# An SSM and FP8 FFN kernel: another cut of the last outputs, another order of the last products

## Chip, cores, metric

The kernel runs on one core of a Trainium2 chip. The metric is device time in microseconds (us). Three runs of the kernel before gave 304.72 to 305.21 us, median 305.06. A core has TensorE (PE, matrix products), VectorE (DVE), ScalarE (ACT), GpSimd (POOL) and SyncE (SP), each with an instruction queue of its own; SP and GpSimd also issue the DMAs, which 16 DMA engines carry out.

## What is computed

x has shape (128, 32, 512): batch, heads, sequence. Each head is convolved along the sequence with a kernel built from state-space parameters, masked by the length of the row, quantised to FP8, sent through a gated feed-forward layer over the sequence axis (512 to 1376 and back), and added to x:

```python
K = 2.0 * einsum('hn,hnl->hl', Ct, exp(P)).real            # (32, 512)
y = irfft(rfft(x, 1024) * rfft(K, 1024))[..., :512] + x * D[:, None]
y = y * (arange(512) < length[:, None])[:, None, :]
h = silu(fp8(y) @ gate_w.T) * (fp8(y) @ up_w.T)            # (128, 32, 1376)
out = x + fp8(h) @ down_w.T
```

(Scales are left out; `fp8` stands for clipping and rounding to float8.)

## The kernel before

The 32 heads are worked on in G = 8 groups of HG = 4. The batch of 128 lies on the partitions, so a group's output is 128 rows of 4 x 512 float32, 1 MB. Each group goes through these stages:

- **Convolution and sorting** (`conv`, `sort`): TensorE convolves with Toeplitz tiles, VectorE scales and masks to `q`, TensorE permutes the batch by length, ScalarE writes `qs`.
- **Gate and up** (`gate_up`): 11 chunks of 128 hidden units (IC = 11). For each, TensorE fills the PSUM tiles `gp` and `up` (L646), ScalarE makes silu (L654), VectorE the product `v` (L656). ScalarE (L621) and VectorE (L622, L623, L624) round it to `hq`. These jobs work on batches of chunks: chunk 0, then 1-2, 3-4, 5-6, 7-8, then 9 and 10 alone. The first jobs run inside `gate_up`, the rest come back in `jobs`.
- **Down** (class `Down`): a unit is a head, or part of a head's 512 columns, and has its own PSUM tile. `multiply(n, i0, i1)` issues unit n's products with chunks i0 to i1 of `hq` (L688). `put_out(n)` lets VectorE add scaled products to `xn`, the group's sorted x (L701), and, if n stands in `self.sent`, issues a scatter of some columns of `xn` to an output tensor: an indirect DMA on GpSimd (L706), with a row number for each partition, since the batch was sorted.

Groups overlap: the products of a group stand between the convolutions of the next. EARLY = 5 and LATE = 9 are chunk numbers. In group g = 6, the last but one, `put_out` runs for heads 0 to 2 in the loop, and head 3 is left over: its products and its `put_out` (`before.put_out(HG - 1)`, L838) stand after the gate and up products of group 7. Group 7 has five units, named `halves`: heads 0, 1 and 2 whole, and head 3 in two halves of 256 columns. Their PSUM tiles carry the tags dp, gp, up, gp, up: four of them reuse buffers of the gate and up products.

The end is written out by hand. After `d` is made for group 7, VectorE finishes the remaining jobs; then `before.put_out(3)` is issued, then TensorE's products in the order of the loops at L839 and L843. Ahead of the last unit's `put_out` stands `verdict`: VectorE compares what was collected in `fin`, `big`, `low` and `fits` (L551 to L555), reduces it (L557, L558), TensorE sums over partitions (L561), and VectorE writes `any_bad` (L562), a flag that says whether the fast path held. Every engine then loads this flag (L922) and branches (L923) over a second arm of the program, `wide()`, which computes everything again in a slower way if the flag is set. With the given inputs the branch passes over it. Line L969 stands for the end of the program: waiting for all DMAs, and barriers between the engines.

The order of an engine's instructions is that of the program, except where `with after(x)` sets one behind x in the scheduling order; waits are put in by the framework from the tiles each instruction reads and writes.

Of the kernel before, what the change touches and what calls it, by code (L numbers as in the profile page):

```python
# [57 lines left out]
def ssm_fp8_ffn(  # L58
# [13 lines left out]
    L, H, B = xT.shape  # L72
# [3 lines left out]
    IC = (I + P - 1) // P  # L76
    IP = IC * P
    NA, NB = 16, 32
    HG = 4
    T = HG * B  # L80
    G = H // HG
# [108 lines left out]
    last = kg.tile([1, NR], F32, name="last")  # L190
# [9 lines left out]
    def after(done):  # L200

        return tc.issue_after(done.ins)
# [361 lines left out]
    def narrow():  # L564
        with ExitStack() as arm:
# [6 lines left out]
            def conv(g, q, j, xg, xs, before):  # L572

                st, loaded = toeplitz(stp, g * HG + j, nc.gpsimd if g == 1 else nc.sync)
                cp, t, convolved, copied = convolve(st, xg, xs, j, inv[:, 0:1], before)
                nc.vector.scalar_tensor_tensor(  # L576
                    q[:, j, :].rearrange("p (k c l) -> p k c l", k=2, c=2),
                    cp.rearrange("p (k c) l -> p k c l", k=2),
                    inv[:, 0:1],
                    t,  # L580
                    ALU.mult,
                    ALU.add,
                    saturate=False,
                )
                words = q.bitcast(I32)[:, j, :]
                made = nc.vector.tensor_tensor(words, words, mask.bitcast(I32), ALU.bitwise_and)  # L586
                return convolved, made, loaded, copied

            def sort(q, qs, j, before):

                pq = ps.tile([P, NQ], F32, name="pq", tag="up")
                for c in range(LC):
                    done = nc.tensor.matmul(  # L593
                        pq[:, OFF[c] : OFF[c] + CAPS[c]],
                        q[:, j, CHUNKS.index(c) * P : (CHUNKS.index(c) + 1) * P],
                        perm[:, 0 : CAPS[c]],
                        start=True,
                        stop=True,
                    )
                with after(before):  # L600
                    return done, nc.scalar.activation(qs[:, j, :], pq, AF.Copy, saturate=False)  # L601
# [68 lines left out]
            LATE = IC - 2  # L670

            class Down:


                def __init__(self, g, hq, xn, units, tags, between=iter(()), some=0):
                    self.g, self.hq, self.xn, self.units, self.tags = g, hq, xn, units, tags
                    self.between, self.some = between, some
                    self.dps = [None] * len(units)

                    n, last = len(units) - 1, (HG - 1) * L  # L680
                    self.sent = [(g, n, 0, HG * L)] if g < G - 1 else [(g, HG - 2, 0, last), (G, n, last, HG * L)]

                def multiply(self, n, i0, i1):
                    j, l0, l1 = self.units[n]
# [78 lines left out]
            halves = [*whole[:-1], (HG - 1, 0, L // 2), (HG - 1, L // 2, L)]  # L763
            for g in range(G):
# [9 lines left out]
                d = Down(g, hq, xn, whole, ["dp", "dp", "cp", "cp"], *some.get(g, ()))  # L774
# [7 lines left out]
                last, sent = multiplied, None  # L782
                for j in range(HG):
# [3 lines left out]
                    with after(last), after(done):  # L787
                        last, done, loaded, sent = conv(g + 1, q, j, xg, xs, sent)
                    if j == 1:
                        for n in range(2):  # L790
                            with after(last):
                                last = d.multiply(n, 0, EARLY)
                    if j >= 2:
                        with after(last):
                            last, sent = sort(q, qs, j - 2, sent)
# [9 lines left out]
                for n in range(2):  # L805
                    with after(last):
                        last = d.multiply(n, EARLY, LATE)
                for n in range(2, HG):
                    with after(last):
                        last, sent = sort(q, qs, n, sent)  # L810
# [5 lines left out]
                with after(last):  # L816
                    last = d.multiply(2, 0, LATE)
                for n in range(HG):
                    if (g, n) == (G - 2, HG - 1):
                        break  # L820
                    with after(last):
                        last = d.multiply(n, LATE if n < 3 else 0, IC)
# [6 lines left out]
            with after(multiplied):  # L829
                last = d.multiply(HG - 1, 0, IC)  # L830
            check_q(G - 1, q)
            before = d
            d = Down(g, hq, xn, halves, ["dp", "gp", "up", "gp", "up"])
# [3 lines left out]
            with after(done):  # L837
                done = before.put_out(HG - 1)  # L838
            for i0, i1 in ((0, EARLY), (EARLY, LATE)):  # L839
                for n in range(3):  # L840
                    with after(last):
                        last = d.multiply(n, i0, i1)
            for n in range(len(halves)):  # L843
                with after(last):
                    last = d.multiply(n, LATE if n < 3 else 0, IC)
                    if n == len(halves) - 2:
                        with after(done):
                            verdict(last)
                d.put_out(n)

    def wide():

        with ExitStack() as arm:
            wp = arm.enter_context(tc.tile_pool(name="wp", bufs=1))
            wp2 = arm.enter_context(tc.tile_pool(name="wp2", bufs=2))
            masks = [wp.tile([P, LC, B], F32, name=f"mask{n}") for n in range(2)]
            for n, m in enumerate(masks):
                build_mask(m, inv[:, n : n + 1])

            def quantise(out, v, F):  # L860

                nc.vector.tensor_scalar(v, v, FP8_MAX, -FP8_MAX, ALU.min, ALU.max)
                m = wp2.tile([P, 4 * T], F32, name="wm")
                nc.scalar.activation(m[:, 0:F], v, AF.Copy, scale=2.0**20)
                mi = m.bitcast(I32)[:, 0:F]
                nc.vector.tensor_scalar(mi, mi, 0x7F800000, 0x00400000, ALU.bitwise_and, ALU.bitwise_or)
                nc.vector.scalar_tensor_tensor(v, m[:, 0:F], 1.5 * 2.0**14, v, ALU.max, ALU.add)
                nc.vector.scalar_tensor_tensor(out, m[:, 0:F], 1.5 * 2.0**14, v, ALU.max, ALU.subtract)

            for g in range(G):  # L870
                xg = load_x(g)
                xs = add_chunks(xg)
                xn = xp.tile([P, HG * L], F32, name="xn", bufs=2)
                nc.sync.dma_start(xn, xb[g])
                qs = [wp.tile([P, LC, T], F32, name=f"wq{n}") for n in range(2)]
                for j in range(HG):
                    cp, t = convolve_wide(toeplitz(wp, g * HG + j)[0], xg, xs, j, wp2)
                    y, y1 = (q[:, :, j * B : (j + 1) * B] for q in qs)
                    nc.vector.tensor_copy(y[:, 0:2, :], cp[:, 0:2, :])
                    nc.vector.tensor_add(y[:, 2:4, :], cp[:, 2:4, :], t.unsqueeze(1).to_broadcast([P, 2, B]))  # L880
                    nc.vector.tensor_mul(y1, y, masks[1])
                    nc.vector.tensor_mul(y, y, masks[0])
                for q in qs:
                    y = q.rearrange("p c t -> p (c t)")
                    quantise(y, y, LC * T)
                hq = wp.tile([P, IC, T], F32, name="whq")
                for i in range(IC):
                    gp = ps.tile([P, T], F32, name="gp")
                    up = ps.tile([P, T], F32, name="up")
                    for o, w, q in ((gp, gw, qs[0]), (up, uw, qs[1])):  # L890
                        for c in range(LC):
                            nc.tensor.matmul(
                                o,
                                w[:, c, i * P : (i + 1) * P],
                                q[:, c, :],
                                start=(c == 0),
                                stop=(c == LC - 1),
                            )
                    s = wp2.tile([P, T], F32, name="ws", bufs=1)
                    v = wp2.tile([P, T], F32, name="wv", bufs=1)  # L900
                    nc.scalar.activation(s, gp, AF.Silu, scale=ngate)
                    nc.vector.scalar_tensor_tensor(v, up, nup, s, ALU.mult, ALU.mult)
                    quantise(hq[:, i, :], v, T)
                for j in range(HG):
                    dp = ps.tile([P, L], F32, name="dp")
                    for i in range(IC):
                        nc.tensor.matmul(
                            dp,
                            hq[:, i, j * B : (j + 1) * B],
                            dw[:, i, :],  # L910
                            start=(i == 0),
                            stop=(i == IC - 1),
                        )
                    o = xn[:, j * L : (j + 1) * L]
                    nc.vector.scalar_tensor_tensor(o, dp, ndown, o, ALU.mult, ALU.add)
                l0 = 0
                for o in outs[g : g + 1] if g < G - 1 else outs[g:]:
                    nc.sync.dma_start(o, xn[:, l0 : l0 + o.shape[1]])
                    l0 += o.shape[1]

# [2 lines left out]
    with tc.If(bad > 0):  # L923
        wide()
# [49 lines left out]
```

## Time and profile before

| What | Value |
|---|---|
| median of 3 runs | 305.06 us |
| profiled execution: its time | 305.09 us |
| its span, first to last instruction | 303.2 us |
| TensorE busy | 283.9 us, 94% of the span |
| VectorE busy | 264.3 us, 87% |
| ScalarE busy | 181.0 us, 60% |
| GpSimd busy | 50.8 us, 17% |
| mean granted TensorE clock | 0.986 |
| written to memory / read | 8.54 MB / 39.03 MB |
| scatters of the output (L706) | 9, about 1.0 us on GpSimd each |

The busy share of an engine is an average over stages with different limits. Times inside the execution count from the start of the span. Engine names with a q (PEldq, SPq) are sequencer entries: branches, semaphore waits, drains, which are not counted as busy. In a row of the timeline, `x11` says that 11 instructions of one kind were merged, and brackets give the idle time before them and what ended it.

### The profile page before, as it was taken

The page shows a single profiled execution, that of the slowest core. Times are in us where ns is not written, and L with a number is a line of the kernel's source. Part 1 is how long each engine was busy: PE and PEld are TensorE (multiplying, and loading weights), DVE is VectorE, ACT ScalarE, POOL GpSimd, SP SyncE. Part 2 cuts the span into 40 slices and gives each one's busy share as a digit, 9 for nine tenths or more (in the row PEclk, how much of TensorE's full clock was granted, in tenths as well). Part 3 has the DMA queues.
Part 4 walks back from the last instruction along what each step waited for, and adds up shares of the span by engine and source line. Part 5 has one row for each costly group of instructions (what it writes and reads, how often), then busy time and mean ns, then how long its engine had stood idle before and what let it go on. Part 6 is the DMA issues. An engine that isn't in the chain of part 4 may idle for free.

```text
span 303.2 us, 4843 instructions
## 1 busy us (share of the span) xinstructions
PE 283.9 (94%) x1708; PEld 171.3 (57%) x1708; DVE 264.3 (87%) x466; ACT 181.0 (60%) x385; POOL 50.8 (17%) x104
## 2 busy tenths in 40 slices
PE   8889999997999999999999999999999999999850
PEld 3467567454774557645774567555774567455330
DVE  5875999989999999969997899969996999899960
ACT  4964783877729783658726782748533881579200
POOL 5771340210002100130002100310003200000030
PEclk9999999999999999999999999999999999999995
DMA  2599999981069602792059404890259430000052
GB/s 83 192 261 381 378 361 341 256 278 44 20 128 243 271 1 50 193 316 111 22 129 311 201 1 89 248 304 21 58 148 294 175 125 0 0 1 3 0 214 72
DMA packets 26039, 47.95 MB, mean 158 GB/s; under 512 B 2848, under 2 KB 15404, under 8 KB 24088
## 3 DMA queue, kind: packets, MB, share of 16 engines
q1 hardware_dynamic: 21784, 26.28, 28.9%
q0 software_dynamic: 4224, 21.29, 20.8%
q8 instruction: 15, 0.25, 0.3%
q14 instruction: 16, 0.13, 0.2%
HBM read 39.03 MB, written 8.54 MB: 157 GB/s over the span
## 4 chain that ended last, share of the span: by engine, by line
DVE 44%; PE 29%; issue 12%; ACT 8%; DMA 3%; SPq 1%; POOL 1%; POOLq 0%; ACTq 0%
PE dp L688 11%; DVE v L656 10%; DVE v L622 10%; DVE hq L623 9%; PE gp L646 5%; DVE q L576 5%; ACT s L654 5%; PE up L646 4%; DVE hq L624 4%; ACT m L621 2%; DMA st<-kpad 2%; PE cp L497 1%; PE cp L495 1%; PE cp L496 1%; DVE q L586 1%
## 5 line engine op out<-in xcount | busy, mean ns | idle before, releaser
L688 PE MATMUL dp<-dw,hq 128*128 128x512 bf16 (+1 forms) x363 | 84.6, 380 | 3.1 <-DVE hq L624 2.5
L654 ACT ACTIVATE s<-gp,psc 128x512 f32<-128x512 f32 x88 | 58.5, 680 | 30.7 <-PE gp L646 30.3
L646 PE MATMUL up<-qs,uw 128*128 128x512 fp8e4 (+1 forms) x352 | 70.3, 321 | 2.3 <-DVE v L656 1.8
L656 DVE SCALAR_TENSOR_TENSOR v<-up,psc,s 128x512 f32<-128x512 f32 x88 | 64.3, 745 | 7.7 <-ACT s L654 7.7
L646 PE MATMUL gp<-qs,gw 128*128 128x512 fp8e4 (+1 forms) x352 | 70.4, 321 | 0.6 <-ACT qs L601 0.6
L688 PEld LDWEIGHTS <-hq 128*128 128x128 bf16 x363 | 33.2, 96 | 44.5 <-DVE hq L624 7.5
L623 DVE SCALAR_TENSOR_TENSOR hq<-m,v 128x1024 bf16<-128x1024 bf16 (+1 forms) x56 | 55.5, 991 | 1.1
L622 DVE SCALAR_TENSOR_TENSOR v<-m,v 128x1024 f32<-128x1024 bf16 (+1 forms) x56 | 55.4, 989 | 1.2 <-ACT m L621 1.2
L621 ACT ACTIVATE m<-v 128x1024 bf16<-128x1024 f32 (+1 forms) x56 | 48.7, 870 | 8.9 <-DVE v L656 8.9
L646 PEld LDWEIGHTS <-uw 128*128 128x128 bf16 x352 | 32.0, 97 | 28.9 <-issue 3.8
L646 PEld LDWEIGHTS <-gw 128*128 128x128 bf16 x352 | 31.9, 97 | 26.4 <-issue 0.7
L601 ACT ACTIVATE qs<-pq 128x376 fp8e4<-128x376 f32 x32 | 14.6, 480 | 30.3 <-PE pq L593 30.3
L701 DVE SCALAR_TENSOR_TENSOR xn<-dp,nsc,xn 128x512 f32<-128x512 f32 (+1 forms) x33 | 23.0, 729 | 9.0 <-PE dp L688 8.8
L493 ACT ACTIVATE shared<-sp,inv 128x128 f32<-128x128 f32 x32 | 11.3, 360 | 27.6 <-PE sp L490 27.6
L576 DVE SCALAR_TENSOR_TENSOR q<-cp,inv,shared 128x512 fp8e4<-128x512 f32 x32 | 23.8, 744 | 2.1 <-PE cp L499 1.5
L111 POOL DMA_DIRECT2D xs<-xT x6 | 3.5, 586 | 116.4 <-PE sp L490 116.4
L706 POOL DMA_INDIRECT out<-xn,index x9 | 9.5, 1060 | 76.8 <-DVE xn L701 72.4
L624 DVE TENSOR_SCALAR hq<-hq 128x1024 bf16<-128x1024 bf16 (+1 forms) x56 | 20.9, 373 | 1.4
L495 PE MATMUL cp<-st,xg 128*128 128x256 f32 x64 | 19.2, 381 | 0.0
L497 PE MATMUL cp<-st,xg 128*128 128x256 f32 x64 | 19.1, 380 | 0.0
L496 PE MATMUL cp<-st,xg 128*128 128x256 f32 x64 | 19.0, 379 | 0.0
L607 ACT ACTIVATE s<-q 128x1024 bf16<-128x1024 fp8e4 x16 | 16.7, 1054 | 0.0
(159 smaller groups left out, 283.7 us busy)
## 6 DMA issues: line engine op xcount, KB each, us to landing
xg<-xT SPq DMA_DIRECT2D x8, 1024.0 KB, 7.7
st<-kpad SPq DMA_DIRECT2D x28, 192.0 KB, 3.8
st<-kpad SPq DMA_DIRECT2D x28, 128.0 KB, 3.5
xs<-xT POOLq DMA_DIRECT2D x12, 256.0 KB, 4.6
dw<-downT SPq DMA_DIRECT2D x2, 1280.0 KB, 19.3
gw<-gateT SPq DMA_DIRECT2D x2, 768.0 KB, 8.6
gw<-gateT SPq DMA_DIRECT2D x1, 1216.0 KB
uw<-upT SPq DMA_DIRECT2D x1, 1216.0 KB
```

Source lines behind the costliest of these rows:

```text
L495: nc.tensor.matmul(cp[:, 1:4:2, :], xg[:, 0, b], st[:, 2:4, :], start=True, stop=False)
L497: nc.tensor.matmul(cp[:, 1:3, :], xg[:, 1, b], st[:, 3:5, :], start=False, stop=False)
L576: nc.vector.scalar_tensor_tensor(q[:, j, :].rearrange("p (k c l) -> p k c l", k=2, c=2), cp.rearrange("p (k c) l -> p k c l", k=2), inv[:, ...
L621: nc.scalar.activation(m, v, AF.Abs, scale=2.0**20 * (1.0 + 2.0**-6), accum_out=acc)
L622: yield nc.vector.scalar_tensor_tensor(v, m, 1.5 * 2.0**14, v, ALU.max, ALU.add)
L623: yield nc.vector.scalar_tensor_tensor(out, m, 1.5 * 2.0**14, v, ALU.max, ALU.subtract)
L624: yield nc.vector.tensor_scalar(out, out, FP8_MAX, -FP8_MAX, ALU.min, ALU.max)
L646: multiplied = nc.tensor.matmul(o[:, :, 0 : CAPS[c]], w[:, c, i * P : (i + 1) * P], qs[:, :, OFF[c] : OFF[c] + CAPS[c]], start=(c == 0), s ...
L654: gated = nc.scalar.activation(s, gp, AF.Silu, scale=pgate)
L656: done = nc.vector.scalar_tensor_tensor(v[:, (i - i0) * T : (i - i0 + 1) * T], up, pup, s, ALU.mult, ALU.mult)
L688: done = nc.tensor.matmul(self.dps[n], self.hq[:, i, j * B : (j + 1) * B], dm[:, i, l0:l1], start=(i == 0), stop=(i == IC - 1),)
L701: added = nc.vector.scalar_tensor_tensor(o, self.dps[n], ndown, o, ALU.mult, ALU.add)
```

## The change

Two things change.

First, group 6 (g = G - 2) sends its output in two scatters, as group 7 does already: three heads after `put_out(2)`, one head after `put_out(3)`. The output tensors are cut accordingly: ten and not nine, the last four with the widths of 3, 1, 3 and 1 heads. The reference's shape is put together from them afterwards on the host, as before.

Second, in the last group the two half units of the last head join the others in the loop over chunks 0 to 4 and 5 to 8, so that their products with these chunks are issued before any unit's products with chunks 9 and 10. Before, all eleven products of each half stood at the very end.

```diff
-                    self.sent = [(g, n, 0, HG * L)] if g < G - 1 else [(g, HG - 2, 0, last), (G, n, last, HG * L)]
+                    k = g + max(0, g - (G - 2))
+                    self.sent = [(k, HG - 2, 0, last), (k + 1, n, last, HG * L)] if g >= G - 2 else [(g, n, 0, HG * L)]
...
             for i0, i1 in ((0, EARLY), (EARLY, LATE)):
-                for n in range(3):
+                for n in range(len(halves)):
                     with after(last):
                         last = d.multiply(n, i0, i1)
             for n in range(len(halves)):
                 with after(last):
-                    last = d.multiply(n, LATE if n < 3 else 0, IC)
+                    last = d.multiply(n, LATE, IC)
                     if n == len(halves) - 2:
                         with after(done):
                             verdict(last)
...
-                for o in outs[g : g + 1] if g < G - 1 else outs[g:]:
+                for o in outs[g : g + 1] if g < G - 2 else outs[2 * g - G + 2 :][:2]:
...
-    widths = [*(v.shape[1] for v in groups[:-1]), 3 * L, L]
+    widths = [*(v.shape[1] for v in groups[:-2]), 3 * L, L, 3 * L, L]
```

In the built program TensorE's and VectorE's queues hold as many instructions as before. On TensorE, 18 products of 256 columns stand further ahead. On VectorE one pair changes places: the last `put_out` stands ahead of L558 and no longer behind it. GpSimd's queue has one scatter more. The other edits change only the arm that is branched over.

## The prediction

> **What bounds it now.** I start at the end, with the chain of waits in order of time. Columns: start and length in us, engine and what it worked on.
>
> ```profile
> 289.21 0.05 issue
> 289.26 3.81 PE dp L688 x27
> 293.07 0.02 issue
> 293.09 0.48 DVE xn L701
> 293.57 0.07 DVE any_bad L562
> ...
> 293.66 0.68 POOLq L922
> 294.34 0.48 POOL out L706
> ```
>
> VectorE's last piece of `hq` releases 27 matmuls, then the last `put_out`, the verdict and the last scatter. This chain ends at 294.82, but the span is 303.2: 8.4 us have no arithmetic in them. The chain cannot say what fills them, so I look at the sequencers, by line L923 (the branch over the wide arm) and L969 (the end of the program), and at SP's waits.
>
> ```profile
> L923 PEldq COMPARE_BRANCH  x1: 4538/4538/4538, 294.4 to 294.4; - x1
> ...
> L969 PEldq DRAIN  x2: 8/8/8, 302.4 to 302.7; - x2
> L969 POOLq DRAIN  x3: 46/109/6357, 294.7 to 303.0; - x3
> ...
> SPq L969 <- DMA out<-xn,index: 3.7, 2, 2.2
> SPq L969 <- PEq L969: 2.9, 2, 2.4
> ```
>
> TensorE's sequencer needs 4.54 us for its branch, goes on at 299.0, and reaches its drain only at 302.4 (VectorE and ScalarE go on at 299.2 and 299.3, and have theirs right after). SP has seen every scatter land by 300.2 and then waits up to 2.4 us for TensorE; GpSimd's long drain ends at 301.05. So **TensorE's instruction stream ends the kernel**, not the scatters. Next, the stretches after the arithmetic. Columns: from and to, length, busy time and count of PE, PEld, DVE, ACT, POOL, then clock, DMA share, GB/s.
>
> ```profile
> 291.70:294.30 2.60, 1.50 (x14) 0.99 (x12) 1.75 (x11) 0.00 (x0) 1.42 (x2) 1.00 0.99 403
> 294.30:296.50 2.20, 0.00 (x0) 0.00 (x0) 0.00 (x0) 0.00 (x0) 0.53 (x1) 0.67 0.97 376
> 296.50:297.50 1.00, 0.00 (x0) 0.00 (x0) 0.00 (x0) 0.00 (x0) 0.00 (x0) 0.50 0.79 217
> ...
> 299.00:299.80 0.80, 0.00 (x0) 0.00 (x0) 0.00 (x0) 0.00 (x0) 0.00 (x0) 0.50 0.00 0
> ```
>
> The DMA engines are full from 291.7 to 296.5: the 1 MB of group 6 until 294.3, the 0.75 MB of three heads of group 7 behind it, then the last 0.25 MB. The packet records put one 16 KB packet of the instruction queue q8 at 296.56 to 297.47, and a second at 299.82 to 301.03. Of the first branch (issued 294.43): 2.13 us to its packet, 0.91 of packet, 1.50 more. Of the second fetch (after the semaphore that ended at 299.08): 0.74, 1.21, 1.38, on idle DMA engines. So the first waits some 1.4 us for scatters. That two branch targets outside the instruction memory cost fetches is what the Trainium skill says ("Runtime: NRT & Kernel Launch", Instruction fetch mechanics).
>
> Last, TensorE, VectorE and GpSimd around the final products, from the timeline:
>
> ```profile
> 285.95 2.66 PE L688 MATMUL dp<-dw,hq 128*128 128x512 bf16 x11 [1.45 <-DVE hq L624]
> 289.12 2.72 DVE L701 SCALAR_TENSOR_TENSOR xn<-dp,nsc,xn 128x512 f32<-128x512 f32 x4
> ...
> 292.11 0.97 POOL L706 DMA_INDIRECT out<-xn,index  x1 [0.97 <-DVE xn L701]
> 292.13 0.47 DVE L701 SCALAR_TENSOR_TENSOR xn<-dp,nsc,xn 128x256 f32<-128x256 f32 x1
> 292.53 0.24 DVE L557 TENSOR_REDUCE bad<-ok 128x1 f32<-128x95 f32 x1
> 292.80 0.15 DVE L558 TENSOR_SCALAR bad<-bad 128x1 f32<-128x1 f32 x1
> ```
>
> VectorE is busy without a gap from 289.12 to 292.77, whatever TensorE does meanwhile.
>
> **Part 1, 18 products moved.** Both half units (256 columns) do chunks 0 to 8 before chunks 9 and 10 of any unit. The starts of successive matmuls lie 0.227 us apart at 512 columns and 0.113 at 256; the 28 that start at 278.0 end their issue at 284.35, and the next waits until 285.95 for chunks 7 and 8. Ten half products (1.13 us) go into that hole of 1.6. The eight others follow the ten 512-wide ones (285.95 + 2.27 = 288.22) until 289.13; chunk 9 of unit 0 then ends its issue at 289.36, 0.10 after `hq` is complete at 289.26. Five wide and four half ones follow: 5 x 0.227 + 4 x 0.113 = 1.59, so TensorE is through at 290.95 plus 0.16 of pipeline, 291.1 and not 293.05: **1.9 us earlier**. PSUM buffers cost nothing: the last reader of `gp` ends at 279.1, of `up` at 279.9.
>
> Almost none of it reaches the end. VectorE's four `put_out` start at 289.12 by its own queue; the one that could be late, unit 0, has its product at 289.75 and is due at 289.78. The five verdict comparisons and `put_out` 3 are VectorE-bound too. In the built order the last `put_out` now stands ahead of L558: it starts at about 292.69 and not 293.09 (**0.40 earlier**), L558 moves from 292.80 to about 293.09, its tiny matmul to 293.30, `any_bad` from 293.49 to 293.55: **0.05 later**. Every branch waits for `any_bad`, so this part alone gives +0.05 on that chain. The last scatter, behind `put_out`, is issued 0.40 earlier (293.45; GpSimd is free at 293.08).
>
> **Part 2, group 6 in two scatters.** GpSimd gets one more DMA of 0.97 us, at about 265.3, after the three `put_out` that end at 264.99; nothing else is in its queue until 290, nothing waits behind it. Its 0.75 MB move at 267 to 269 while the DMA share is at most 0.02. Upper bound for the neighbours: in 234.8 to 238, under the scatter of the group before, VectorE's L656 takes 750 ns, ScalarE's L654 688, TensorE's L646 321; in the quiet 266.9 to 270 they take 748, 685 and 321. Six such operations of VectorE and ScalarE: under 0.02 us. I take 0.
>
> The rule against it: the Trainium skill prices one GpSimd DMA at about 2.0 us plus bytes / 436 GB/s ("DMA: Bandwidth & Descriptors", Anatomy of one DMA), so cutting 1 MB in two adds 2 us. The rows give 5.1 to 5.8 us to landing, so a fixed part is real, but the new piece's lies 24 us before anyone needs it, and the remaining 0.25 MB at 290.15 is followed by longer ones. By the rule summed on the path +2.0, by the rows 0.
>
> What it removes: 6 of 8 KB of every row of that first scatter. Its data began 1.56 us after issue (291.71) and ran to 294.35; now 0.66 us of it, to about 292.4. The three-head scatter is issued at 292.11 as before. If it too needs 1.56 us, it begins at 293.68 and not behind the backlog at 294.35: **0.67 earlier**, and ends as much earlier. That latency is the one unknown: this trace has one scatter on idle DMA engines to show it; the gathers L464 show 2.1 to 2.7 in other stages. At 2.24 or more nothing is gained; below 1.56 nothing speaks. I take 1.56, the row of the same operation in the same place.
>
> **What the fetch waits for.** The skill has each DMA engine alternate between queues after a packet of some 9 to 17 descriptors (same page, Queues, rings and completion order). The row: due at about 294.43 + 0.74 = 295.2, the fetch began at 296.56, directly after the semaphore write that ends the 8 rows of the three-head scatter on its engine. If a packet is one row (0.25 us), the rule would have let it in by 295.4, the backlog would cost nothing, and part 2 would give 0. If a packet is those nine descriptors, rule and row agree, and the fetch starts 0.67 earlier. I follow the row.
>
> **Sum.** Fetch 1 from 296.56 to 295.89: -0.67. What follows, to the second fetch and the end, is fixed (5.8 us), perhaps less the 0.1 by which 1.50 exceeds 1.38 under lighter load; I take -0.03. The +0.05 of `any_bad` vanishes in the wait that remains (295.2 to 295.9). In all -0.70. The profiled execution took 305.09: span 303.2 and 1.9 around it; it stands 0.03 above the median. **Forecast 304.4 us**, -0.22%. Next behind TensorE is GpSimd's drain (301.05 against 302.41): it caps any gain at 1.36, 303.7.
>
> **Rivals.** (1) Nothing at the end, **305.05**: the last scatter, issued 0.40 earlier, is ready at 293.45 + 1.56 = 295.0, ahead of the fetch (295.2), where it was ready at 295.4, after it. If engines serve by arrival, four packets of 0.17 us go first and eat the 0.67. [...]Against: two of the four instruction packets of 296.6 got in after a single packet of that scatter. (2) **Slower, 305.7**: the same overtaking while the three-head scatter starts later than 293.7, in the worst case at 294.35 as now, because the latency after issue, not the backlog, set it. Then the fetch starts at 296.56 + 0.67 = 297.2, +0.65. It decides from 293.7 on: earlier, the shift is a gain. For it: the gathers' latencies; against: its first packet lay within 0.01 us of the end of the first scatter's data. That the change would not do what it says is no rival: the built order has both halves' products ahead of the last chunks, and both scatters.
>
> **Chances.** Forecast 0.53 (own range 304.1 to 304.7), rival 1 0.23, rival 2 0.24. With about 0.2% (0.6 us) as what a measurement of this kernel can tell: faster takes four fifths of the forecast's cases, 0.44; the rest of it and most of rival 1, 0.31; slower, rival 2 and a little, 0.25. The range 303.8 to 305.7 goes down nearly to the cap and up to rival 2.
>
> **What would show it.** TensorE's L688 at 291.1, last `put_out` at 292.7, `any_bad` near 293.55; a three-head scatter at 265.3; the middle scatter's first data at 293.7; q8's packet at 295.9; the branch near 3.8 us; TensorE's drain near 301.7. A branch of 4.5 us or more speaks for rival 1 or 2; with `any_bad` later than 293.7, or VectorE's work up to 289.2 longer than now, the forecast is wrong at its root.

## The result and the profile after

The changed kernel took 304.6 us in the median of 20 runs (303.65 to 306.05), the kernel before 305.1 us beside it. The ratio is 0.9985, with an interval of 0.9973 to 0.9996: **0.15% faster**, some 0.46 us of the 0.70 that were forecast. Two further timings of the same kernel (below) gave 0.9999 (0.9985 to 1.0012) and 1.0000 (0.9979 to 1.002). Weighted by their intervals the three give 0.9992, give or take 0.0008, or 0.23 us; the kernel before, timed against itself, gave 0.9993 (e8). So the gain is smaller than forecast, and the times alone hardly tell it from none. What the change does is read from the profiles.

The profiled execution took 304.11 us, with a span of 302.3. That is 0.98 below the profiled execution of before, but 0.65 of it has nothing to do with the change: by 27 us, long before anything that was changed, this execution is 0.65 ahead. From there to 289 us every one of VectorE's instructions starts 0.63 to 0.67 us earlier than its partner of before; in another profile of the same kernel they start 0.69 to 0.73 later. So I count the end from the **end of VectorE's last `hq` operation** (289.20 before, 288.56 after).

The sequencers' records of the changed kernel, by line (the branch is now L924, the end L970), and SP's waits:

```profile
L924 PEldq COMPARE_BRANCH  x1: 3938/3938/3938, 294.3 to 294.3; - x1
...
L970 POOLq DRAIN  x3: 46/103/5169, 294.6 to 302.0; - x3
L970 PEldq DRAIN  x2: 8/8/8, 301.4 to 301.8; - x2
...
SPq L970 <- PEq L970: 3.3, 2, 2.8
SPq L970 <- DMA out<-xn,index: 2.4, 1, 2.4
```

The branch is 0.60 us shorter (3.94 against 4.54), and TensorE's drain, at 301.4, is still what SP waits for last. The same view for the flag's load, L922 before and L923 after, shows something that the forecast did not have:

```profile
L922 PEldq TENSOR_LOAD <-any_bad x1: 659/659/659, 293.7 to 293.7; - x1
```

```profile
L923 PEldq TENSOR_LOAD <-any_bad x1: 1109/1109/1109, 293.1 to 293.1; - x1
```

The load of `any_bad` takes 0.45 us longer, so the branch begins 0.48 later, counted from `hq`. The stretches of the changed kernel (from and to, length, busy time of PE, PEld, DVE, ACT, POOL, clock, DMA share, GB/s):

```profile
291.00:291.90 0.90, 0.00 (x0) 0.00 (x0) 0.90 (x8) 0.00 (x0) 0.42 (x1) 1.00 0.77 291
291.90:293.00 1.10, 0.19 (x2) 0.09 (x2) 0.82 (x5) 0.00 (x0) 0.74 (x2) 1.00 0.00 0
293.00:295.10 2.10, 0.00 (x0) 0.00 (x0) 0.01 (x1) 0.00 (x0) 0.77 (x1) 1.00 0.98 388
```

The small scatter of group 6 is through by 291.9. The DMA engines then stand idle for 1.1 us until the three-head scatter begins, at the moment when the flag is loaded (its first data at 293.00, the load from 293.05). Before, they had no such gap. The timeline of TensorE, VectorE and GpSimd (the scatter of 264.62 is the extra one):

```profile
285.31 5.15 PE L689 MATMUL dp<-dw,hq 128*128 128x512 bf16 x27 [0.32 <-DVE hq L624]
```

```profile
291.89 0.24 DVE L557 TENSOR_REDUCE bad<-ok 128x1 f32<-128x95 f32 x1
292.05 0.47 DVE L702 SCALAR_TENSOR_TENSOR xn<-dp,nsc,xn 128x256 f32<-128x256 f32 x1
292.44 0.14 DVE L558 TENSOR_SCALAR bad<-bad 128x1 f32<-128x1 f32 x1
292.87 0.15 DVE L562 TENSOR_SCALAR any_bad<-bp 1x1 int32<-1x1 f32 x1 [0.28 <-PE bp L561]
```

```profile
264.62 0.99 POOL L707 DMA_INDIRECT out<-xn,index  x1 [23.68 <-DVE xn L702]
289.49 0.98 POOL L707 DMA_INDIRECT out<-xn,index  x1 [23.88 <-DVE xn L702]
291.48 0.96 POOL L707 DMA_INDIRECT out<-xn,index  x1 [1.01 <-DVE xn L702]
292.80 0.97 POOL L707 DMA_INDIRECT out<-xn,index  x1 [0.36 <-DVE bad L558]
```

TensorE's products end at 290.46, 1.90 after `hq`, where they ended 3.85 after it. VectorE has the last `put_out` 0.40 earlier and `any_bad` 0.02 later (4.31 against 4.29).

### The profile page after: what moved, and what is told of

Same layout as the page of the kernel before. It is cut to its first block, busy times and chain, and to the rows that moved or that the text cites. A ratio compares the mean times of both kernels' runs of the same rounds, so it can differ in the third digit from the quotient of the medians.

```text
span 302.3 us, 4827 instructions
## 1 busy us (share of the span) xinstructions
PE 282.8 (94%) x1691; PEld 171.6 (57%) x1708; DVE 264.3 (87%) x466; ACT 180.9 (60%) x385; POOL 51.1 (17%) x105
## 4 chain that ended last, share of the span: by engine, by line
DVE 45%; PE 28%; issue 12%; ACT 8%; DMA 3%; SPq 1%; POOL 1%; ACTq 0%; POOLq 0%
DVE v L656 11%; DVE v L622 11%; PE dp L689 10%; DVE hq L623 10%; PE gp L646 5%; DVE q L576 5%; ACT s L654 5%; PE up L646 4%; DVE hq L624 4%; ACT m L621 2%; DVE xn L702 2%; DMA st<-kpad 2%; PE cp L497 1%; PE cp L495 1%; PE cp L496 1%
## 5 line engine op out<-in xcount | busy, mean ns | idle before, releaser
L689 PE MATMUL dp<-dw,hq 128*128 128x512 bf16 (+1 forms) x347 | 81.1, 380 | 2.5 <-DVE hq L624 0.8
L493 ACT ACTIVATE shared<-sp,inv 128x128 f32<-128x128 f32 x32 | 11.3, 360 | 27.6 <-PE sp L490 27.6
L707 POOL DMA_INDIRECT out<-xn,index x10 | 10.5, 1051 | 75.4 <-DVE xn L702 71.9
```

The source lines that it names most:

```text
L689: done = nc.tensor.matmul(self.dps[n], self.hq[:, i, j * B : (j + 1) * B], dm[:, i, l0:l1], start=(i == 0), stop=(i == IC - 1),)
```

## Experiments

All times in this table are us after the end of VectorE's last `hq`, read from the traces, except two durations: the flag's load and the branch, both of TensorE. "Fetch" is the start of the 16 KB packet on the instruction queue q8 that follows TensorE's first branch; "landing" is the last count of the last scatter's semaphore; TensorE's drain is its first DRAIN entry at the end of the program; the tail reaches to the end of the span. Line numbers shift by a few with each edit. In the cuts of code, `...` stands for what is left out, and comments are mine.

| Kernel | flag's load | fetch | branch | landing | TensorE's drain | tail | time ratio (interval) |
|---|---|---|---|---|---|---|---|
| before | 0.66 | 7.36 | 4.54 | 10.24 | 13.21 | 14.05 | |
| before again (e8) | 0.66 | 7.36 | 4.90 | 10.32 | 13.06 | 13.90 | 0.9993 (0.9981 to 1.0004) |
| changed | 1.11 | 6.69 | 3.94 | 9.52 | 12.87 | 13.71 | 0.9985 (0.9973 to 0.9996) |
| changed again (e3) | 1.10 | 6.71 | 3.44 | 9.35 | 12.54 | 13.37 | 0.9999 (0.9985 to 1.0012) |
| changed, third (e11) | 1.11 | 6.97 | 3.78 | 9.18 | 13.01 | 13.85 | 1.0000 (0.9979 to 1.002) |
| products only (e1) | 0.62 | 7.76 | 4.92 | 10.21 | 13.53 | 14.36 | 1.0017 (1.0003 to 1.0031) |
| scatters only (e2) | 1.09 | 6.81 | 3.58 | 9.26 | 12.81 | 13.64 | 0.9992 (0.9972 to 1.0011) |
| no last scatters (e4) | 0.49 | 6.03 | 3.60 | none | 12.24 | 13.08 | one execution |
| products only, held (e7) | 0.64 | 7.35 | 4.52 | 10.16 | 12.79 | 13.63 | 0.9991 (0.998 to 1.0003) |
| early flag (e5) | 0.48 | 2.31 | 3.88 | 9.30 | 9.29 | 11.79 | 0.994 (0.9922 to 0.9957) |
| early flag, products late (e6) | 0.49 | 3.32 | 3.78 | 9.39 | 9.58 | 11.88 | 0.9936 (0.9919 to 0.9953) |
| early flag on before (e9) | 0.49 | 5.69 | 5.92 | 9.99 | 11.65 | 12.49 | 0.9957 (0.9937 to 0.9977) |
| early flag, cut 2 and 2 (e10) | 0.48 | 2.98 | 4.10 | 8.05 | 9.76 | 10.60 | 0.9891 (0.9871 to 0.9911) |
| the same, products late (e12) | 0.49 | 3.31 | 3.44 | 9.68 | 9.23 | 12.17 | 0.9935 (0.9913 to 0.9958) |

Two profiles of one kernel do not agree in everything. The fetch starts within 0.01 us where the backlog sets it (before, e8, e7) and within 0.28 in the changed kernel, but the branch differs by up to 0.50 and the tail by up to 0.48.

**e1, the products alone.**

```diff
# on the kernel before
-                for n in range(3):
+                for n in range(len(halves)):
...
-                    last = d.multiply(n, LATE if n < 3 else 0, IC)
+                    last = d.multiply(n, LATE, IC)
```

> Only the products are moved; group 6 keeps its one scatter of 1 MB. Theory (TensorE's first instruction fetch waits for the scatter rows queued ahead of it, and the scatters' backlog is unchanged): last put_out about 0.40 us earlier, any_bad within 0.1 us of before, first branch of TensorE 4.3 to 4.8 us, time ratio 0.999 to 1.001. Rival (engines serve strictly by arrival, so the earlier last scatter goes ahead of the fetch): branch about 5.2 us and the time 0.5 to 0.7 us above before (ratio 1.002). Rival (the products are what gained): ratio 0.9985.

The first rival: the fetch moved from 7.36 to 7.76, the branch took 4.92, and the kernel became slower by 0.17%, 0.5 us. The last scatter, issued at 4.25 and not 4.65, went ahead of the fetch, which starts directly after the first of that scatter's semaphore writes (7.75). By itself, this part of the change costs time.

**e2, the scatters alone.** The changed kernel with the loops of before:

```diff
-                for n in range(len(halves)):
+                for n in range(3):
...
-                    last = d.multiply(n, LATE, IC)
+                    last = d.multiply(n, LATE if n < 3 else 0, IC)
```

> Only group 6's output is cut in two scatters; the products stay at the end. Theory (backlog): the middle scatter's data begins 0.67 us earlier than before, counted from VectorE's last hq; the fetch's packet too; TensorE's first branch 3.8 to 4.0 us and the time 0.4 to 0.8 us below before (ratio 0.9975 to 0.9987). Rival (the cut buys nothing, the products did it): ratio 1.000, branch 4.5 us.

The three-head scatter's data began at 4.44 (5.15 before), the fetch at 6.81, the branch took 3.58: the mechanism is there. The branch is shorter than expected (3.8 to 4.0), and the time, 0.9992, cannot be told from no change, nor from the range expected: its interval holds both.

**e3 and e11, the changed kernel again.**

> The changed kernel once more, to see which of its profile's numbers repeat: the 1.1 us load of the flag (0.66 us before), the branch of 3.9 us, and the 0.65 us that its first 27 us were shorter. Theory: the branch repeats within 0.3 us, the early 0.65 us does not (it is the luck of the first loads), the flag's load follows the load on the DMA engines and stays near 1.1. Rival: the flag's load is chance and comes back near 0.66. Ratio 0.9973 to 0.9996 again.

> The changed kernel a third time, for its size: two timings gave 0.9985 and 0.9999 with intervals of 0.0012 on either side. Theory (the fetch starts 0.65 us earlier and some of it is lost after that): ratio 0.9985 to 0.9995, fetch at 6.7 us after the last hq, flag's load 1.1 us. Rival (it gains nothing): 0.9995 to 1.0005.

The branch repeats within 0.5 us (3.94, 3.44, 3.78), not within the 0.3 expected, the fetch within 0.28, the flag's load within 0.01; the early 0.65 us does not repeat. The flag's load is therefore not chance. Both timings are higher than the first one, and both lie where the rival of e11 has them, "it gains nothing".

**e4, without the last scatters.** Head 3 of group 6 and all of group 7 are not written.

```diff
-                        if n == n1:
+                        if n == n1 and (self.g < G - 2 or (self.g, n) == (G - 2, HG - 2)):
```

> The changed kernel without its last three scatters (head 3 of group 6 and all of group 7 are not written), so that the DMA engines are idle at the end. Theory (the fetch waits for scatters): TensorE's first branch falls to 3.1 to 3.4 us, like the second fetch, the flag's load to about 0.65 us, and the end comes 0.8 to 1.3 us earlier than in the changed kernel, counted from VectorE's last hq. Rival (the branch is slow by itself): branch 3.9 us or more, the end moves by less than 0.3 us.

Between the two: with idle DMA engines the branch still takes 3.60 and the tail 13.08, 0.3 to 0.8 below the changed kernel's three. So, as far as one profile tells, no arrangement of the scatters in front of this branch saves much more than 0.9 us of the 13.98 (mean of two) of before; with packets as short as before's two profiles had (2.19 together in the mean, here 2.54) it might be 1.25, by my estimate. It also corrects a figure of mine: on idle engines the first fetch starts 0.94 after the branch (0.97 in e5, 1.05 in e6), not 0.74.

**e7, the products alone, with the last scatter held back.** On e1:

```diff
                         if n == n1:
+                            if hold and (self.g, n) == (G - 1, len(self.units) - 1):
+                                nc.gpsimd.tensor_copy(held, hold[0])   # hold[0] is any_bad
...
```

> e1 (only the products moved) with the last scatter held back on GpSimd until any_bad is written, by a small copy of the flag, so that it is issued near 4.8 us after the last hq and not 4.25. Theory (in e1 the last scatter, issued 0.40 us earlier, went ahead of TensorE's fetch): the fetch starts at about 7.4 us as before, the branch is back near 4.5 us, tail near 14.0, ratio 0.999 to 1.001. Rival (e1 is slower for another reason): fetch at 7.7 to 7.8, branch 4.9, ratio 1.0017 as e1.

As the theory has it: with the last scatter issued at 4.86, the fetch is back at 7.35 and the ratio at 0.9991, where e1 had 1.0017. Their records of the branch, e1 first:

```profile
L923 PEldq COMPARE_BRANCH  x1: 4918/4918/4918, 294.5 to 294.5; - x1
```

```profile
L929 PEldq COMPARE_BRANCH  x1: 4518/4518/4518, 294.4 to 294.4; - x1
```

The two profiles show the overtaking and its end. That it is what made e1 slower, the timings support but do not prove: their intervals meet at 1.0003. The tail, 13.63, lies below the 14.0 expected.

**e8, the kernel before as an experiment.**

> The kernel before, submitted as a kernel: ratio 1.000 within its interval, which shows what the timing can tell, and a second profile of it: flag's load near 0.65 us, first fetch at 7.3 to 7.5 us after the last hq, branch 4.3 to 4.7 us, tail 13.8 to 14.2. Rival (these are one profile's chance): load near 1.1 us or branch below 4.0.

Ratio 0.9993 for the same kernel: this timing tells about 0.1% at best. The branch of 4.90 lies outside what I had expected, by the luck of the packet (1.27 us in place of 0.91).

**e5, the flag early.** The verdict leaves the end: GpSimd compares (the last two comparisons at 280.9 and 282.1, after idling since 266); ScalarE sums; TensorE's product stands ahead of chunk 9; VectorE writes the flag after the leftover head of group 6.

```diff
+            judged = judge()          # 5 comparisons on GpSimd, 1 sum on ScalarE
             with after(done):
                 done = before.put_out(HG - 1)
...
+            last = verdict(last, *judged, done)   # product, any_bad = sum too small
             for n in range(len(halves)):
                 with after(last):
                     last = d.multiply(n, LATE, IC)
-                    if n == len(halves) - 2:
-                        with after(done):
-                            verdict(last)
```

> The changed kernel with the verdict taken off the end: GpSimd makes the five comparisons and ScalarE sums them as soon as h is known, TensorE's small product stands ahead of chunks 9 and 10, VectorE writes any_bad right after head 3 of group 6. Theory (TensorE's instruction stream, from the flag through two fetches, ends the kernel): TensorE branches as soon as its products are done, about 2.7 us after VectorE's last hq and not 5.7, its first fetch starts before the three-head scatter's data and is not held, the flag's load is near 0.5 us, TensorE's drain comes near 10 us after the last hq and not 12.5 to 12.9; then GpSimd's drain (last landing plus 1.6 us) ends the kernel, tail 11.3 to 12 us, time ratio 0.991 to 0.995. Rival (the last scatter's landing sets the end already): tail above 13 us, ratio 0.997 or more.

**0.6% faster than before.** Sequencer records of e5:

```profile
L928 PEldq COMPARE_BRANCH  x1: 3878/3878/3878, 290.2 to 290.2; - x1
...
L974 POOLq DRAIN  x3: 46/109/6378, 293.4 to 300.4; - x3
L974 PEldq DRAIN  x2: 8/8/8, 298.2 to 300.1; - x2
```

TensorE branches at 290.2, 1.3 us after `hq` and not the 2.7 expected (e6 shows why), and its drain comes at 298.2, below GpSimd's, which begins at 293.4 and lasts 6.38, to 299.8. The end has changed hands. GpSimd's drain ends 1.65 us after the last landing, as it does, within 0.05, in every row of the table that has one.

**e6, the same with the products late** (e2's diff on e5).

> The same early flag, but with the half units' products at the very end as before (two scatters for group 6). Theory: now TensorE's own last product (3.9 us after the last hq) holds its branch, its fetch is due behind the three-head scatter again and starts near 6.7 us, tail near 13 us, ratio 0.997 to 0.999: the moved products are worth about 1.5 us once the flag no longer stands behind them. Rival (TensorE does not matter): same time as e5.

Here my theory was wrong and the rival right: ratio 0.9936, as e5. The flag's load and the timeline of TensorE in e6:

```profile
L927 PEldq TENSOR_LOAD <-any_bad x1: 486/486/486, 291.1 to 291.1; - x1
```

```profile
289.44 3.80 PE L694 MATMUL dp<-dw,hq 128*128 128x512 bf16 x27 [0.42 <-DVE hq L629]
```

TensorE's sequencer loads the flag at 291.1, while its products run until 293.24. The sequencer hands products on well ahead of the array, so the branch does not wait for the last of them: late products cost it 0.9 us (2.27 against 1.34), while the products themselves end 1.7 later (3.86 against 2.13).

**e9, the early flag on the kernel before**, with its single 1 MB scatter:

> The early flag alone, put on the kernel before: one scatter of 1 MB for group 6, half units' products at the end. Theory (with the flag early, the last landing plus 1.65 us ends the kernel, and the backlog of 0.75 MB delays that landing): last landing near 10.1 us after the last hq and not 9.3, GpSimd's drain near 11.8, tail 12.5 to 12.8, ratio 0.995 to 0.998, some 0.7 us above e5 and e6. Rival (the cut of group 6 is worth nothing either): ratio 0.994 as e5.

Ratio 0.9957 and tail 12.49, as expected. The tail is 0.7 above e5's; the times do not separate the two, since their intervals overlap. Its branch is the clearest sight of the wait in this study:

```profile
L927 PEldq COMPARE_BRANCH  x1: 5918/5918/5918, 291.3 to 291.3; - x1
```

```profile
291.60:294.20 2.60, 1.30 (x12) 0.86 (x9) 1.06 (x3) 0.00 (x0) 1.46 (x2) 1.00 1.00 400
294.20:294.80 0.60, 0.00 (x0) 0.00 (x0) 0.00 (x0) 0.00 (x0) 0.47 (x1) 1.00 0.95 365
```

The first packet of q8 after the branch lies in the stretch from 294.7 to 295.7 (in the row: packets, MB, share of 16 engines):

```profile
q8 instruction: 1, 0.02, 6.1%
```

The branch is issued at 2.27 and on idle engines its fetch would begin at about 3.24 (2.27 + 0.97). The 1 MB scatter has held the DMA engines since 2.57, eight rows of 0.32 us on each. The fetch begins at 5.69, after the last of them, 2.4 us late. It did not get in between two rows. That speaks against one of the forecast's two readings, in which a fetch waits for a single row, and for the one in which it waits for all eight.

**e10, the early flag and the last group cut two and two.** On e5:

```diff
+                    cut = 2 if g == G - 1 else HG - 1
-                    self.sent = [(k, HG - 2, 0, last), (k + 1, n, last, HG * L)] if g >= G - 2 else [(g, n, 0, HG * L)]
+                    self.sent = [(k, cut - 1, 0, cut * L), (k + 1, n, cut * L, HG * L)] if g >= G - 2 else [(g, n, 0, HG * L)]
...
-    widths = [*(v.shape[1] for v in groups[:-2]), 3 * L, L, 3 * L, L]
+    widths = [*(v.shape[1] for v in groups[:-2]), 3 * L, L, 2 * L, 2 * L]
```

> e5 with the last group's output cut two heads and two, not three and one (group 6 stays three and one): its first scatter can be issued one put_out earlier and the last one is no longer behind 0.75 MB. Theory (last landing sets the end): last data by 6.7 to 7.3 us after the last hq and not 8.8, GpSimd's drain near 9.0, then TensorE's drain (9.3 in e5) takes over, tail 10.0 to 10.6, ratio 0.987 to 0.991. Rival (the fetches hold the last scatter's packets on their engines until 8.5 us whatever its place): tail 11.4 or more, ratio 0.993 or more.

301.86 us, **1.1% faster than before, the best of the study**. Its records:

```profile
L975 POOLq DRAIN  x3: 46/109/4890, 293.6 to 299.2; - x3
L975 PEldq DRAIN  x2: 8/8/8, 298.6 to 298.9; - x2
```

GpSimd's drain ends at 298.5 (293.64 + 4.89), TensorE's comes at 298.6: both limits now lie together. The fetches still meet scatters. The branch is issued at 1.34 as in e5, but the first fetch begins at 2.98 and not 2.31, with the small scatter of group 6 under way since 2.56. The second begins 1.91 after the branch has ended (1.66 in e5), where it took 0.72 to 0.85 in every kernel with the flag late.

**e12, the same with the products late** (e2's diff on e10).

> e10 with the half units' products back at the very end, to see what the move is worth once neither the flag nor a backlog stands behind it. Theory (the moved products bring the last put_out, and so the last scatter, forward; TensorE's branch does not wait for them): last scatter issued near 4.65 us after the last hq and not 3.93, its landing about 8.5 and not 8.05, GpSimd's drain near 10.2 against TensorE's 9.8, tail 10.9 to 11.3, ratio 0.990 to 0.993. Rival (the move is worth nothing here either): tail 10.6, ratio as e10 (0.987 to 0.991).

Without the moved products the last scatter is issued at 4.66 and not 3.93, lands at 9.68 and not 8.05, and 0.4% is lost (0.9935 against 0.9891; the intervals are just apart, and each kernel was timed beside its own runs of before). The landing is later than I expected (8.5), and so is the tail (12.17, not 10.9 to 11.3). Fifteen of the 16 counts of the last scatter's semaphore are in by 8.33; the last engine's rows run until 9.21. By the times, the second fetch (6.66 to 7.92) stood in front of them; the trace does not name the engine of a packet.

## Where the prediction was right, and where not

**What ends the kernel** was right: TensorE's stream, from the flag through two fetches. e5 shows it by taking the flag away from the end.

**Part 1** was right step by step: products 1.95 us earlier (forecast 1.9), last `put_out` and last scatter 0.40 earlier (0.40), `any_bad` 0.02 later (0.05), nothing of it at the end. Alone it even costs 0.17%, by the overtaking that I had put into rivals 1 and 2.

**Part 2** was right in the transfer: the extra scatter at 264.6 leaves no trace in VectorE's starts (none of the 2.0 us by which the rule set against the rows would have lengthened the path), and the three-head scatter begins 0.71 earlier (0.67), so 1.56 us was the right latency.

**The fetch** was forecast 0.67 earlier. The three profiles have it at 6.79 in the mean, against 7.36: 0.57. The reason for it is only half the one I gave. In the changed kernel the backlog no longer holds the fetch: the three-head scatter's rows are all through by 6.54. The branch at 5.71 plus 0.97 is 6.68, so in two of the three profiles (6.69, 6.71; e11 has 6.97) the fetch comes when the branch lets it, and the branch is 0.48 later by the flag's load, 0.45 longer. That term stood nowhere in my sum.

**The term that failed in size** is "what follows, to the second fetch and the end, is fixed", with -0.03. From the fetch's start to the end it is 6.62 in the mean of two profiles of before (6.69, 6.54), 6.85 in three of the changed kernel (7.02, 6.66, 6.88): +0.23. It took back two fifths of the 0.57. So the profiles show -0.33 at the end in place of -0.70, and the three timings -0.23 with about as much of uncertainty.

Nearly all of the +0.23 lies in the two packets of 16 KB themselves. Together they take 2.12 and 2.26 us in the two profiles of before, 2.31 to 2.55 in the three of the changed kernel (+0.21 in the mean); the rest of the stretch is the same within 0.03. With the flag late, all four profiles without the cut of group 6 lie at 1.88 to 2.26, and all five with it at 2.31 to 2.65. The scatters are not the reason, for e4 has 2.54 on idle engines. With the flag early the pattern breaks: 1.88 in e10 with the cut, 2.41 in e9 without. Whether this is a cost of the change or the spread of fetches is open.

**Luck.** The first timing, 304.6, lies in the forecast's own range (304.1 to 304.7), but it is the best of three, and together they give a third of the forecast's 0.70. The mechanism holds without it; the closeness of the number is in part luck. A slip in the chances changes nothing of this: four fifths of 0.53 is 0.42, not 0.44.

**Rivals.** Rival 1's overtaking is real in e1, and goes away in e7. In the changed kernel it did not show, although its last scatter is issued at 4.25 too: the fetch started 0.21 to 0.49 after the first row of that scatter, not 0.67. Why it was passed by a whole scatter in e1 and not here was not settled. Rival 2's condition, a three-head scatter later than 293.7, did not come about.

## To carry to other kernels

When a span ends several microseconds after the last arithmetic, read the sequencers' records first: a branch there is a chain of flag, load and instruction fetches, and moving the flag forward onto idle engines (0.4% alone in e9, 0.6% with the change in e5) was worth more than reordering the work in front of it (0.15% at most). The best kernel needed both the early flag and a cut that brings the last scatter forward (e10, 1.1%). In these runs a fetch waited behind scatters already queued, so a cut that clears the queue and an order that issues a scatter earlier work against each other. The same move of products cost 0.17% (e1), was worth nothing (e6 against e5) and was worth 0.4% (e12 against e10), by what stood behind it.

## What the runs showed of the hardware

- An instruction fetch that fell due while a scatter of 8 rows on each DMA engine ran began after its last row: 2.4 us late in e9, about 1.2 in the kernel before (7.36 against 5.23 + 0.97). In e1 it waited for a second scatter as well (7.76). It is no rule without exception: in the changed kernel the fetch began 0.21 to 0.49 us after the first row of the last scatter, whose rows take 0.67 on an engine.
- TensorE's load of the flag took 0.48 to 0.49 us with idle DMA engines (e4 and the five kernels with the flag early), 0.62 to 0.66 under a running scatter (before, e1, e7, e8), and 1.09 to 1.11 in all four profiles in which a scatter's first rows started together with it (changed, e3, e11, e2). The cause was not tried, and no rule comes out of it: in e9 VectorE's load took 1.28 us, begun 1.3 us after the first row of the 1 MB scatter.
- TensorE's sequencer reached the flag's load 2.2 us before its array had finished the products in front of it (e6).
- GpSimd's drain at the end of the program ends 1.6 to 1.7 us after the last landing of its scatters.
